# A two-layer graph network on one core: counts and column numbers in separate PSUM banks, one bank for transposes, own rows read a group earlier and transposed ahead of the sums

## The chip, the cores and the metric

The kernel runs on one core of a Trainium2 chip. The metric is the device time of one execution in microseconds (us); lower is better. The kernel is written so that the order of instructions on each engine is the order in the program; semaphores between the engines are put in by the framework wherever two instructions touch the same tile.

The core has a matrix engine (TensorE, "PE"), a vector engine (VectorE, "DVE"), a scalar engine (ScalarE, "ACT"), a general engine that here issues the indirect transfers (GpSimd, "POOL") and one that issues the plain transfers (SyncE, "SP"). TensorE writes into PSUM, which this kernel uses as eight banks of 128 partitions by 512 floats.

## The reference, cut to what matters

There are 6250 nodes with 512 floats each and 106250 directed edges `(src, dst)`: 50000 random pairs in both directions and a loop on every node, sorted by `dst`. Two layers follow each other:

```
layer 0:  out = segment_sum((x @ W_l.T + b_l)[src], dst) / max(deg, 1) + x @ W_r.T
          h   = layernorm(x + out)
layer 1:  msg = h[dst] @ W_neigh.T + b_neigh
          neigh = segment_sum(msg, src) / max(deg, 1)
          out = relu(h @ W_self.T + b_self + neigh)
          y   = layernorm(h + out) * gamma + beta
          result = layernorm(h + y)
```

Since the projection is linear, the kernel averages the neighbours' rows first and multiplies the average with the weights afterwards. Layer 1 sums by `src`, so its edges have to be sorted anew.

## The kernel before, in words

**Tiles and groups.** A layer's sorted edges are cut into 831 tiles of 128. Seven tiles (`SPAN`) form a window, which ends within 64 nodes (`H`); there are `NW` = 119 windows, and a visit to an eighth tile (`VIS` = 8), the last one of the window before, collects the edges at the border. A group `g` handles two windows, `g` and `Q + g` with `Q` = 60, in the lower and upper 64 partitions. The function `grouped` handles one layer with a loop over the groups and is called twice, for layer 0 with table `x` and for layer 1 with table `h_d`.

**The steps of a group**, with the lines of their instructions:

- `fetch(g)`: 14 indirect transfers on GpSimd (L478), each bringing the 128 rows of one tile, 256 KB, into `rows`. There are six such buffers of seven tiles, that is for three groups; the last tile of a group is read once more by the first sums of the next.
- `match(g)`: one VectorE instruction (L497, recorded at helper line L170) builds `hot`, which says for each edge of each visit which of the 64 nodes it belongs to, by comparing with the column numbers 0 to 63. These numbers lie in PSUM, in the first 64 columns of the tile `misc`.
- `shrink(g)`: ScalarE copies `hot` to the narrower type bf16, `hotb` (L504).
- `own_rows(g)`: SyncE loads two row numbers into registers (L509) and issues two transfers of the nodes' own rows into `own` (L543). In one group of layer 0 GpSimd gathers them.
- `visits(g)`: 16 TensorE matmuls sum the rows of each node in `agg` (L555).
- `count(g)`: eight small matmuls (L565) count the edges of each node, into column 64 or 65 of `misc`; VectorE forms `inv` and `some` from it (L438, L439, L441).
- `average(g)`: ScalarE multiplies `agg` by `inv` into `mean` (L574).
- `dense(g)`: 16 matmuls (L456) with both weights into `po`, of which there is one.
- `turn(g)`: TensorE transposes the own rows and then the averages, four blocks each (L447), into tiles `tp`, of which there are two; ScalarE copies each to `ownT` or `meanT` (L449).
- `store(g)`: the bias, the normalization and, in layer 1, the rest of the formula on VectorE (from L414 in layer 0, from L424 in layer 1; one square root on ScalarE, L406), then two transfers of the result by SyncE (L598).

**The order.** The program order of the loop sets the order on every engine. In round `g` it is: fetch and match of `g + 1`; own rows, visits, count and average of `g`; dense of `g - 1`; turn of `g`; store of `g - 1`; shrink of `g + 1`. In layer 0 the call `more` puts steps of the sort for layer 1 between these (five a round on VectorE, after the shrink; those with TensorE transposes after the average); groups 0 to 43 or so carry them, groups 44 to 59 none. Layer 1 has no such steps.

**PSUM.** The banks of a layer are one for `misc`, two for `tp`, two for `agg`, one for `po`, and two of the sort.

**Another path.** A function `plain` is there for edge lists that don't fit the windows. It uses the same `transposed` and doesn't run with these inputs.

Of the kernel before, what the change touches and what calls it, by code (L numbers as in the profile page):

```python
# [9 lines left out]
F32 = mybir.dt.float32  # L10
# [3 lines left out]
ALU = mybir.AluOpType  # L14
# [4 lines left out]
P = 128  # L19
H = 64  # L20
SPAN = 7
VIS = SPAN + 1
# [74 lines left out]
def kernel(  # L97
# [16 lines left out]
    nc = tc.nc  # L114
    N, D = x.shape
    E = src.shape[0]
    NK = D // P
# [16 lines left out]
    iota = const.tile([P, P], F32, name="iota")  # L134
# [33 lines left out]
    def both(o, a, b, op):  # L168

        nc.vector.scalar_tensor_tensor(o, a, 1.0, b, op0=ALU.mult, op1=op)  # L170
# [265 lines left out]
    def inverse(deg, nr, work):  # L436
        inv = work.tile([P, 1], F32, name="inv")
        nc.vector.tensor_scalar(inv[:nr], deg, 1.0, None, op0=ALU.max)  # L438
        nc.vector.reciprocal(inv[:nr], inv[:nr])  # L439
        some = work.tile([P, 1], F32, name="some")  # L440
        nc.vector.tensor_scalar(some[:nr], deg, 1.0, None, op0=ALU.min)  # L441
        return inv, some

    def transposed(v, nr, name, work, ps):
        p = ps.tile([P, NK, P], F32, name="tp", bufs=2)
        for k in range(NK):
            nc.tensor.transpose(p[:, k, :nr], v[:nr, k * P:(k + 1) * P], ident[:nr, :nr])  # L447
        t = work.tile([P, NK, P], F32, name=name)
        nc.scalar.copy(t[:, :, :nr], p[:, :, :nr])  # L449
        return t  # L450
# [9 lines left out]
    def grouped(s, table, w_n, w_s, layer, finish, dest, other, sps):  # L460


        with tc.tile_pool(name=f"g{layer}", bufs=2) as work, tc.tile_pool(
            name=f"gp{layer}", bufs=2, space=PSUM
        ) as ps:
            chunks, hots, state = {}, {}, {}
            misc = ps.tile([P, H + 2], F32, name="misc", bufs=1)
            nc.vector.tensor_copy(misc[:, :H], iota[:, :H])  # L468

            def halves(g):  # L470
                return [c for c in range(2) if c * Q + g < NW]

            def tiles(g, c):
                w = c * Q + g
                return range(w * SPAN, min(M, (w + 1) * SPAN))

            def gather(t, m):
                nc.gpsimd.indirect_dma_start(  # L478
                    out=t, out_offset=None, in_=table,
                    in_offset=bass.IndirectOffsetOnAxis(ap=s.idx[:, m:m + 1], axis=0))  # L480

            def fetch(g):
                if g == 0:

                    first = work.tile([P, D], F32, name="mean")
                    gather(first, Q * SPAN - 1)
                    chunks[-1, 1] = {Q * SPAN - 1: first}
                for c in halves(g):
                    t = work.tile([P, SPAN, D], F32, name="rows", bufs=CHUNKS)
                    chunks[g, c] = {}  # L490
                    for i, m in enumerate(tiles(g, c)):
                        gather(t[:, i, :], m)
                        chunks[g, c][m] = t[:, i, :]

            def match(g):
                hot = work.tile([P, VIS * 2, H], F32, name="hot")
                both(hot, s.rel[:, g].rearrange("p v c -> p (v c)").unsqueeze(2)  # L497
                     .to_broadcast([P, VIS * 2, H]),
                     misc[:, :H].unsqueeze(1).to_broadcast([P, VIS * 2, H]), ALU.is_equal)
                hots[g] = hot  # L500

            def shrink(g):
                hb = work.tile([P, VIS * 2, H], BF16, name="hotb", bufs=1)
                nc.scalar.copy(hb, hots[g])  # L504
                hots[g] = (hots[g], hb)

            def start(w, t):

                return nc.values_load(  # L509
                    s.lo_i[:1, w:w + 1], engines=[ENG.SP], min_val=0, max_val=t.shape[0] - H,  # L510
                    skip_runtime_bounds_check_because="the windows hold: N - H at most, or N "
                    "in a table of N + 128")

            def slots(g, beyond):

                n = H * len(halves(g))
                r = work.tile([P, 1], F32, name="r")
                for c in halves(g):
                    a, w = H * c, c * Q + g
                    nc.vector.tensor_scalar(r[a:a + H], slot[a:a + H], s.lo[a:a + H, w:w + 1],  # L520
                                            None, op0=ALU.add)
                    if beyond:
                        far = work.tile([P, 1], F32, name="far")
                        nc.vector.tensor_scalar(far[a:a + H], r[a:a + H],
                                                s.lo[a:a + H, w + 1:w + 2], FAR,
                                                op0=ALU.is_ge, op1=ALU.mult)
                        both(r[a:a + H], r[a:a + H], far[a:a + H], ALU.add)
                if not beyond:
                    nc.vector.tensor_scalar(r[:n], r[:n], float(N - 1), None, op0=ALU.min)
                i = work.tile([P, 1], I32, name="ri")  # L530
                nc.vector.tensor_copy(i[:n], r[:n])
                return i

            def own_rows(g):
                own = work.tile([P, D], F32, name="own")
                n = H * len(halves(g))
                if g == NW - 1 - Q and table.shape[0] < NP:
                    nc.gpsimd.indirect_dma_start(
                        out=own[:n], out_offset=None, in_=table,
                        in_offset=bass.IndirectOffsetOnAxis(ap=slots(g, False)[:n, :1], axis=0))  # L540
                    return own
                for c in halves(g):
                    nc.sync.dma_start(own[H * c:H * (c + 1)],  # L543
                                      table[ds(start(c * Q + g, table), H), :])
                return own

            def visits(g):
                agg = state[g]["agg"] = ps.tile([P, D], F32, name="agg")
                hot = hots[g][0]
                for v in range(VIS):  # L550
                    for c in halves(g):
                        w = c * Q + g
                        first, end = (1 if w == 0 else 0), 1 + len(tiles(g, c))
                        if first <= v < end:
                            nc.tensor.matmul(  # L555
                                agg[H * c:H * (c + 1), :], hot[:, 2 * v + c, :],
                                chunks[g if v else g - 1, c][w * SPAN + v - 1],
                                start=(v == first), stop=(v == end - 1))

            def count(g):  # L560
                st, hb = state[g], hots[g][1]
                nr = st["nr"]
                st["deg"] = misc[:, H + g % 2:H + g % 2 + 1]
                for v in range(VIS):
                    nc.tensor.matmul(st["deg"][:nr],  # L565
                                     hb[:, 2 * v:2 * v + nr // H, :].rearrange("p c h -> p (c h)"),
                                     ones_b, start=(v == 0), stop=(v == VIS - 1))
                st["inv"], st["some"] = inverse(st["deg"][:nr], nr, work)

            def average(g):  # L570
                st = state[g]
                nr = st["nr"]
                mean = work.tile([P, D], F32, name="mean")
                nc.scalar.mul(mean[:nr], st["agg"][:nr], st["inv"][:nr])  # L574
                st["mean"] = mean

            def turn(g):
                st = state[g]
                for v in ("own", "mean"):
                    st[v + "T"] = transposed(st[v], st["nr"], v + "T", work, ps)  # L580

            def dense(g):
                st = state[g]
# [21 lines left out]
            def more(count, tensor):  # L605

                while runs and count and runs[0][0] == tensor:
                    runs.pop(0)[1]()
                    count -= 1

            match(0)
            shrink(0)
            fetch(0)
            for g in range(Q + 1):


                if g + 1 < Q:
                    fetch(g + 1)
                    match(g + 1)
                if g < Q:  # L620
                    state[g] = {"nr": H * len(halves(g)), "own": own_rows(g)}
                    visits(g)
                    count(g)
                    average(g)
                    more(1, True)
                if g:
                    dense(g - 1)
                if g < Q:
                    turn(g)
                if g:  # L630
                    store(g - 1)
                if g + 1 < Q:
                    shrink(g + 1)
                more(5, False)
# [138 lines left out]
```

## Time and profile before

| quantity | value |
|---|---|
| median of 3 runs | 2681.61 us (2674.11 to 2683.77) |
| the profiled execution | 2719.07 us, its span 2717.3 us |
| granted TensorE clock in it, mean | 0.899 |
| PE, weight loads, DVE, ACT, POOL busy | 76%, 32%, 39%, 14%, 59% of the span |
| bytes moved | 508 MB, 187 GB/s on average |
| layer 0, groups with the sort (94 to 1045 us) | PE busy 755.5 of 950.7 us, clock 0.89 |
| layer 0, groups without (1063 to 1306 us) | PE busy 205.2 of 242.3 us, clock 0.99 |
| layer 1 (1433 to 2632 us) | PE busy 949.4 of 1199.5 us, clock 0.91 |

The profile follows one execution. Busy times are of the engines' own instructions, so an engine that is not busy may wait for a semaphore, issue a transfer or have nothing to do. In a group of instructions the number in the first column after the bar is their busy time in us, the next the mean of one in ns; after the second bar stands the idle time just ahead of them and what ended most of it. In a list of waits, each row names the waiting engine, what it was about to write, the instruction that released it, and the sum in us, the count and the longest. In the timeline, a row has the start and the busy time in us, the engine, the line and the operation; in square brackets stands the idle time ahead of it with its releaser.

### The profile page before, as it was taken

To read this page: it belongs to the slowest core of one execution; us is meant where nothing else is said; L and a number is where in the kernel's file an instruction comes from. 1 tells how busy PE (TensorE), PEld (TensorE's weight loads), DVE (VectorE), ACT (ScalarE), POOL (GpSimd) and SP (SyncE) were. 2 spreads that over 40 slices of the span, in tenths; PEclk is the share of its full clock that TensorE was granted. 3 is DMA by queue.
4 is the path that set the end of the run, shared out by engine and by line. 5 is a ranking of instruction groups with operands and counts; after the bars stand their busy time and mean duration, and the time that the engine had idled before them with its cause. 6 is when DMAs were issued, how large, how long until landed. Compare 5 with 4: busy or idle time off the path is not lost.

```text
span 2717.3 us, 23134 instructions
## 1 busy us (share of the span) xinstructions
PE 2071.7 (76%) x7807; PEld 861.5 (32%) x7807; DVE 1047.1 (39%) x2139; ACT 390.2 (14%) x685; POOL 1594.0 (59%) x1679
## 2 busy tenths in 40 slices
PE   2488887778787878888927777778777887877785
PEld 1133333333333333333303333333333333333332
DVE  1344434443434443222302444444444444444444
ACT  0111111111111111111101111111111111111111
POOL 4566665556666565666265566665666666656650
PEclk8789988888898989999968998999899899988998
DMA  7576766666666666676366666666666666666650
GB/s 225 164 204 192 204 199 187 184 182 190 190 191 192 184 196 185 196 214 207 106 178 175 189 192 199 202 201 197 187 202 199 203 200 187 195 189 196 202 174 19
DMA packets 177784, 508.07 MB, mean 187 GB/s; under 512 B 35564, under 2 KB 38054, under 8 KB 177646
## 3 DMA queue, kind: packets, MB, share of 16 engines
q0 software_dynamic: 133456, 437.13, 55.5%
q1 hardware_dynamic: 41358, 63.76, 7.3%
q10 hardware_dynamic: 2832, 5.51, 0.6%
q8 instruction: 66, 1.08, 0.2%
q14 instruction: 72, 0.59, 0.1%
HBM read 475.03 MB, written 31.46 MB: 186 GB/s over the span
## 4 chain that ended last, share of the span: by engine, by line
issue 23%; DVE 9%; PE 8%; SPq 7%; DMA 1%; ACT 1%; another core or an unknown queue 1%; POOLq 0%
PE po L456 6%; SPq L543 4%; SPq L598 2%; DVE po L170 2%; DVE stats L402 2%; SPq L509 2%; DVE po L408 1%; PE tp L447 1%; DVE po L424 1%; DVE po L427 1%; DMA own<-h_d 1%; DVE y L170 1%; PE agg L555 1%; ACT rstd L406 0%
## 5 line engine op out<-in xcount | busy, mean ns | idle before, releaser
L478 POOL DMA_INDIRECT rows<-in_x_dram,idx x831 | 797.0, 959 | 492.3 <-PE agg L555 240.3
L478 POOL DMA_INDIRECT rows<-h_d,idx x831 | 788.7, 949 | 482.5 <-PE agg L555 246.8
L555 PE MATMUL agg<-rows,hot 128*64 128x512 f32 x3792 | 918.2, 613 | 37.9 <-issue 21.7
L456 PE MATMUL po<-wb,ownT 128*128 128x512 f32 x960 | 574.2, 754 | 7.3 <-DVE y L170 6.3
L555 PEld LDWEIGHTS agg<-rows,hot 128*64 128x64 f32 x3792 | 293.8, 140 | 580.4 <-issue 536.8
L456 PE MATMUL po<-wa,meanT 128*128 128x512 f32 x960 | 431.5, 592 | 0.0
L565 PE MATMUL misc<-ones_b,hotb 128*128 128x1 bf16 x960 | 41.5, 164 | 349.1 <-issue 225.7
L456 PEld LDWEIGHTS po<-wb,ownT 128*128 128x128 f32 x960 | 222.2, 243 | 261.3 <-issue 260.1
L424 DVE SCALAR_TENSOR_TENSOR po<-bn,some,po 128x512 f32<-128x512 f32 (+1 forms) x60 | 45.3, 756 | 605.0 <-PE tp L447 264.0
L456 PEld LDWEIGHTS po<-wa,meanT 128*128 128x128 f32 x960 | 181.6, 189 | 234.0 <-issue 234.0
L449 ACT COPY ownT<-tp 128x512 f32<-128x512 f32 x120 | 69.9, 582 | 971.4 <-PE tp L447 497.6
L414 DVE SCALAR_TENSOR_TENSOR po<-bl_t,some,po 128x512 f32<-128x512 f32 (+1 forms) x60 | 45.2, 753 | 406.4 <-PE agg L555 212.9
L574 ACT ACTIVATE mean<-agg,inv 128x512 f32<-128x512 f32 x120 | 82.4, 687 | 788.9 <-DVE some L441 319.6
L438 DVE TENSOR_SCALAR inv<-misc 128x1 f32<-128x1 f32 x120 | 18.9, 158 | 425.7 <-remote 312.2
L170 DVE SCALAR_TENSOR_TENSOR srt<-srt 128x448 f32<-128x448 f32 (+2 forms) x310 | 180.2, 623 | 3.9
L565 PEld LDWEIGHTS <-hotb 128*128 128x128 bf16 x960 | 40.8, 99 | 443.9 <-issue 268.7
L447 PE MATMUL tp<-ident,mean 128*128 128x128 f32 x480 | 77.9, 288 | 123.0 <-ACT mean L574 112.1
L170 DVE SCALAR_TENSOR_TENSOR hot<-rel,misc 128x1024 f32<-128x1024 f32 x120 | 145.2, 1211 | 0.2 <-DVE misc L468 0.2
L447 PE MATMUL tp<-ident,own 128*128 128x128 f32 x480 | 76.0, 276 | 67.5 <-issue 39.3
L504 ACT CAST hotb<-hot 128x1024 bf16<-128x1024 f32 x120 | 123.5, 1029 | 22.6 <-DMA bn<-in_L_gnn_b_neigh_dram 16.1
L406 ACT ACTIVATE rstd<-mv,eps 128x1 f32<-128x1 f32 x180 | 53.0, 295 | 464.0 <-DVE mv L404 343.6
L447 PEld LDWEIGHTS tp<-ident,mean 128*128 128x128 f32 x480 | 58.9, 148 | 131.8 <-ACT mean L574 119.8
(111 smaller groups left out, 841.3 us busy)
## 6 DMA issues: line engine op xcount, KB each, us to landing
own<-h_d SPq DMA_DIRECT2D x119, 128.0 KB
own<-in_x_dram SPq DMA_DIRECT2D x117, 128.0 KB
h_d<-y SPq DMA_DIRECT2D x116, 128.0 KB
out_dram<-y SPq DMA_DIRECT2D x116, 128.0 KB
rows<-in_x_dram,idx POOLq DMA_INDIRECT x831
rows<-h_d,idx POOLq DMA_INDIRECT x831
wa<-in_L_gnn_W_l_dram ACTq DMA_DIRECT2D x1, 1024.0 KB
wb<-in_L_gnn_W_r_dram ACTq DMA_DIRECT2D x1, 1024.0 KB
```

Of the source, the lines that this page charges most:

```text
L170: nc.vector.scalar_tensor_tensor(o, a, 1.0, b, op0=ALU.mult, op1=op)
L402: nc.vector.bn_stats(stats[:nr], v)
L424: nc.vector.scalar_tensor_tensor(po, biases["bn"][:nr], some[:nr], po, op0=ALU.mult, op1=ALU.add)
L447: nc.tensor.transpose(p[:, k, :nr], v[:nr, k * P:(k + 1) * P], ident[:nr, :nr])
L449: nc.scalar.copy(t[:, :, :nr], p[:, :, :nr])
L456: nc.tensor.matmul(po[:nr], a[:, k, :nr], w[:, k, :], start=(i == 0 and k == 0), stop=(i == 1 and k == NK - 1))
L478: nc.gpsimd.indirect_dma_start(out=t, out_offset=None, in_=table, in_offset=bass.IndirectOffsetOnAxis(ap=s.idx[:, m:m + 1], axis=0))
L504: nc.scalar.copy(hb, hots[g])
L543: nc.sync.dma_start(own[H * c:H * (c + 1)], table[ds(start(c * Q + g, table), H), :])
L555: nc.tensor.matmul(agg[H * c:H * (c + 1), :], hot[:, 2 * v + c, :], chunks[g if v else g - 1, c][w * SPAN + v - 1], start=(v == first), st ...
L565: nc.tensor.matmul(st["deg"][:nr], hb[:, 2 * v:2 * v + nr // H, :].rearrange("p c h -> p (c h)"), ones_b, start=(v == 0), stop=(v == VIS - 1))
L574: nc.scalar.mul(mean[:nr], st["agg"][:nr], st["inv"][:nr])
```

## The change

The two parts of `misc` become two tiles, each with a bank of its own: `cols` for the column numbers that `match` reads, and `deg` for the counts. To make room, `tp` has one bank instead of two.

The own rows are asked for one group ahead: a new step `begin(g + 1)` follows `match(g + 1)`, and `own` has three buffers. In SyncE's order the reads of group `g + 1` now stand ahead of the stores of group `g - 1`; they stood behind those before. `turn` is split in two. The own rows of group `g` are transposed ahead of `visits(g)`; the averages are transposed where both were, after `dense(g - 1)`. `mean` has one buffer instead of two, and the single extra tile that a layer reads at its beginning goes into a buffer named `y` instead of `mean`.

```diff
 def transposed(v, nr, name, work, ps):
-    p = ps.tile([P, NK, P], F32, name="tp", bufs=2)
+    p = ps.tile([P, NK, P], F32, name="tp", bufs=1)
...
-            misc = ps.tile([P, H + 2], F32, name="misc", bufs=1)
-            nc.vector.tensor_copy(misc[:, :H], iota[:, :H])
+            cols = ps.tile([P, H], F32, name="cols", bufs=1)
+            nc.vector.tensor_copy(cols, iota[:, :H])
...
-                    first = work.tile([P, D], F32, name="mean")
+                    first = work.tile([P, D], F32, name="y")
...
-                     misc[:, :H].unsqueeze(1).to_broadcast([P, VIS * 2, H]), ALU.is_equal)
+                     cols.unsqueeze(1).to_broadcast([P, VIS * 2, H]), ALU.is_equal)
...
-                own = work.tile([P, D], F32, name="own")
+                own = work.tile([P, D], F32, name="own", bufs=3)
...
-                st["deg"] = misc[:, H + g % 2:H + g % 2 + 1]
+                st["deg"] = ps.tile([P, 1], F32, name="deg", bufs=1)
...
-                mean = work.tile([P, D], F32, name="mean")
+                mean = work.tile([P, D], F32, name="mean", bufs=1)
...
-            def turn(g):
+            def turn(g, v):
                 st = state[g]
-                for v in ("own", "mean"):
-                    st[v + "T"] = transposed(st[v], st["nr"], v + "T", work, ps)
+                st[v + "T"] = transposed(st[v], st["nr"], v + "T", work, ps)
...
+            def begin(g):
+                state[g] = {"nr": H * len(halves(g)), "own": own_rows(g)}
+
             match(0)
             shrink(0)
             fetch(0)
+            begin(0)
             for g in range(Q + 1):
                 if g + 1 < Q:
                     fetch(g + 1)
                     match(g + 1)
+                    begin(g + 1)
                 if g < Q:
-                    state[g] = {"nr": H * len(halves(g)), "own": own_rows(g)}
+                    turn(g, "own")
                     visits(g)
                     count(g)
                     average(g)
                     more(1, True)
                 if g:
                     dense(g - 1)
                 if g < Q:
-                    turn(g)
+                    turn(g, "mean")
                 if g:
                     store(g - 1)
```

## The prediction

> **What bounds the kernel now.** I read the engine shares first, then the costliest groups, the releasers of idle time, and then single groups of edges in the timeline. TensorE is busy 76% of the span and ends no chain alone; GpSimd, which issues the gathers, is busy 59%.
>
> Costliest groups (busy us, mean ns of one; idle us before them, and what ended most of it):
>
> ```profile
> L478 POOL DMA_INDIRECT rows<-h_d,idx x831 | 788.7, 949 | 482.5 <-PE agg L555 246.8
> ...
> L555 PE MATMUL agg<-rows,hot 128*64 128x512 f32 x3792 | 918.2, 613 | 37.9 <-issue 21.7
> ...
> L565 PE MATMUL misc<-ones_b,hotb 128*128 128x1 bf16 x960 | 41.5, 164 | 349.1 <-issue 225.7
> ...
> L449 ACT COPY ownT<-tp 128x512 f32<-128x512 f32 x120 | 69.9, 582 | 971.4 <-PE tp L447 497.6
> ```
>
> A gather is 0.95 us of work and 0.30 of issue, so the 14 of a group need 14 x 1.25 = 17.5 us, and from the first one's start to the last one's end 17.2. The waits by engine (sum us, count, longest) say what the idle GpSimd, ScalarE and TensorE wait for:
>
> ```profile
> ACT ownT L449 <- PE tp L447: 497.6, 56, 10.7
> POOL rows L478 <- PE agg L555: 487.0, 109, 11.8
> DVE inv L438 <- remote: 312.2, 25, 58.8
> PE misc L565 <- DVE hot L170: 122.2, 36, 9.9
> PE tp L447 <- DMA own<-h_d: 27.0, 20, 2.5
> ```
>
> The last two are what the change can take away: the count waits for the match of the next group only because both touch one bank, and the transposes wait for their own rows. The first three don't fit the engines' busy times, and the timeline shows why. A layer 0 group without sorting (start us, busy us):
>
> ```profile
> 1157.42 3.60 PE L456 MATMUL po<-wa,meanT 128*128 128x512 f32 x8
> ...
> 1165.69 0.95 POOL L478 DMA_INDIRECT rows<-in_x_dram,idx  x1 [0.30 <-issue]
> ...
> 1169.46 0.76 DVE L414 SCALAR_TENSOR_TENSOR po<-bl_t,some,po 128x512 f32<-128x512 f32 x1 [13.86 <-PE agg L555]
> 1169.52 0.58 ACT L449 COPY ownT<-tp 128x512 f32<-128x512 f32 x1 [13.19 <-PE agg L555]
> 1169.88 0.94 POOL L478 DMA_INDIRECT rows<-in_x_dram,idx  x1 [3.25 <-PE agg L555]
> ```
>
> The dense sum ends at 1161.0. VectorE, idle and waiting for it alone, answers at 1169.5, when the last gather of the running stream has landed (its issue ended at 1166.6, plus 2.9). ScalarE's copy and the next stream start in the same instant. Following all 109 dense ends: 99 fall inside a stream, and 97 of these are answered only 2.5 us or more after the last gather's end (median 2.96); the ten that fall later are answered in 0.04 us. So **TensorE's completions reach the other engines late while a gather stream runs, and come out when it has landed**. An idle TensorE doesn't release them, as layer 0 with sorting shows:
>
> ```profile
> 806.55 0.34 PE L565 MATMUL misc<-ones_b,hotb 128*128 128x1 bf16 x8 [0.43 <-issue]
> ...
> 816.67 0.95 POOL L478 DMA_INDIRECT rows<-in_x_dram,idx  x1 [0.30 <-issue]
> ...
> 820.60 0.16 DVE L438 TENSOR_SCALAR inv<-misc 128x1 f32<-128x1 f32 x1 [14.09 <-remote]
> 821.04 0.69 ACT L574 ACTIVATE mean<-agg,inv 128x512 f32<-128x512 f32 x1 [19.08 <-DVE some L441]
> 821.79 1.12 PE L447 MATMUL tp<-ident,mean 128*128 128x128 f32 x4 [5.86 <-ACT mean L574]
> ```
>
> The count ends at 806.9, TensorE is idle from 815.9, and the inverse starts at 820.6, 3 us after the last gather's end. A stream itself starts on the first sums of a group, so the period locks to 17.2 + 2.9 + 0.35 = 20.45 us in layer 0 without sorting (20.2 to 20.45 measured); with sorting it is 22.2 and in layer 1 21.4 (starts of groups, averaged).
>
> **What the Trainium skill says.** (1) "Perfetto Trace Analysis", Per-instruction lifecycle (Tensor Engine Instruction): a matmul's end is estimated, and its semaphore update follows PSUM's acknowledgement, outside the window shown. The trace fits: the answer takes 0.04 us at best and 14 at worst. (2) "PSUM — Partial Sum Buffer", PSUM bank collisions: two engines in one bank are ordered by bank, not address. That is the wait "PE misc <- DVE hot" above. (3) "Perfetto Trace Analysis", Optimizing Tensor Performance, Matmuls: independent groups should rotate through banks so that evacuation overlaps the next group. Before, the two transposes run 0.46 us apart (2007.59 and 2008.05 in layer 1); after, one bank serves both. (4) "TensorE: Matmul & The Clock Gate", What's actually happening: an idle window of some 3.4 us halves the clock. The trace agrees: dense matmuls stand 0.43 us apart, and 0.85 after long idle.
>
> **The change part by part.** The instructions are the same in number on every engine; only places and waits change.
>
> *Separate banks.* Layer 1's count loses its wait for the match, which stands on VectorE behind the 8.8 us finish: some 3.5 us of TensorE a group. The new bank for counts waits only for the inverse of the group before, over long ago. Costed at nothing beyond that.
>
> *Own rows one group ahead.* The two reads of the next group and their register loads now stand on SyncE in front of a store instead of behind it; they land 3.6 to 4.5 us after issue, and the third buffer gives them some 20 us. The wait of 0 to 3 us (0.8 to 1 on average in layer 1) goes. The stores come later by two issues, which nothing waits for. Nothing further; without that cover of a period it would be the landing, up to 4.5 us a group. In layer 0's group 58 own rows are one GpSimd gather with index steps on VectorE: once, some 2 us moved, nothing. The averages' single buffer: the older one has been transposed before it is rewritten, nothing.
>
> *Own transposes ahead of the sums, one bank.* Together these two gains would take 4 to 5 us off TensorE's layer 1 group, and 1 more by keeping its clock. But here a wait is added. The own transposes of group g+1 overwrite the bank that holds the mean transposes of g, so TensorE must wait for ScalarE's copy of these. Queued behind the waiting transpose are the sums of g+1, and on their first signal hangs the next stream. The mean transposes end 14 to 16 us into the stream, so their completion is held to its landing. Counted from the stream's first gather:
>
> - stream and landing 17.2 + 2.9 = 20.1
> - copy: answer 0.05, copy 0.58
> - own transposes: answer 0.05; 1.0 after 5 us of idle (0.5 at full clock; 1.12 is the row at 821.79)
> - first sums to their signal: 2.3 at half clock, 1.35 at full (both read from the starts of streams)
>
> The sum is 24.1 at half clock, 22.65 at full. I take 24.0, since the idle of 5 us is longer than what halves the clock. The 56 + 56 periods between groups 1 and 57 of layer 0 and of layer 1 take 1214 + 1199.5 = 2413.5 us before. 112 x 24.0 = 2688, so **+275 us**. What lies outside (layer ends, opening streams, first sort: 306 us) I leave. The profiled execution took 2719.07 us (span 2717.3), above the median of 2681.61 by 37; I add the 275 to each: 2994 and **2957, say 2960**. With 22.65 to 25.0 a period (the upper end where a third of the counts is held too, see below) this case reaches from 2805 to 3070.
>
> Bounds of the unknown: the new wait was never in the trace. From below, it costs a prompt round trip: 0.05 + 0.58 + 0.05 = 0.7 us; from above, the hold to landing for the count as well. I take the hold of one signal, because 97 of 99 dense ends, the ones nearest in place, show it.
>
> **The rivals.**
>
> *The round trip is prompt (ends faster).* If TensorE, stopped at the bank, has its last signal out at once, the trip costs 0.7 us against 4 to 5 saved; TensorE then needs 7.1 (sums) + 0.34 + 7.0 (dense) + 1.0 + 0.7 = 16.1 us and the stream sets 20.45, as in layer 0 without sorting. 112 x 20.45 = 2290, so -123: 2560 (2520 to 2640). For it: counts with 2.5 us of idle TensorE ahead were answered in 0.04. Against it: the row at 820.60. It decides from the point where the copy starts less than 3 us after the mean transposes' end.
>
> *The count is held too (slower still).* Layer 1's idle ahead of the count goes with the match's wait. Of 16 counts without idle ahead, the lag was 1 to 14.5 us, median 7.5, and six were held to the landing. If all are, the inverse starts at 20.1, then 0.45 to the mean, 0.7 for it, 1.1 transposes, then the trip of 4.0: 26.4, with answers 26.8; 112 x 26.8 = 3002, +588: 3270. A third of them gives 25.
>
> *No hold at all.* If the late answers came from the order of work before, GpSimd's 17.5 us become the bound: 1960, -454: 2230 to 2280. Against it: nothing in the change touches the streams.
>
> *It does nothing*: the waits saved and added balance, 2670 to 2690.
>
> **How the numbers follow.** Hold of one signal 0.52 (2960), count held too 0.16 (3070 to 3270), prompt 0.22, no hold 0.06, balance 0.04. A measurement of this kernel can tell about 0.5% from no change. Faster 0.28, same 0.04, slower 0.68. Both signs hold much of the chance: the likeliest one's own range is 2805 to 3070; the range of 2540 to 3100 leaves out the free case, the lowest of the prompt one and most of the held counts, some 0.17.
>
> **What the profile after would show.** Right: a wait of the own transposes for ScalarE's copy of the mean's, 4 to 6 us in some 110 groups; that copy starting about 3 us after the last gather's end; GpSimd idle ended by the first sums of 24.0 - 17.5 = 6.5 us a group, against 487.0/109 = 4.5 now; no wait of the count for the match, none for own rows. Wrong: copies that start at once after the mean transposes, with GpSimd idle of 4 us a group or less.

## The result and the profile after

The changed kernel takes 2983.53 us (2979.9 to 2986.35, four runs) against 2682.36 before (four runs): 1.1129 times as long, with a 95% interval of 1.1103 to 1.1155. Its profiled execution took 2986.35 us, the span is 2984.5, and the mean granted clock fell from 0.899 to 0.849. Times here are medians of all runs and ratios are of the fast runs alone, which matters for one kernel below, where 4 of 19 runs lay over 1.5% above its fastest.

The costliest groups of the page of the changed kernel, to be held against those of before:

```profile
L478 POOL DMA_INDIRECT rows<-h_d,idx x831 | 787.3, 947 | 622.4 <-PE agg L555 386.5
L555 PE MATMUL agg<-rows,hot 128*64 128x512 f32 x3792 | 1072.9, 723 | 7.3 <-DMA rows<-h_d,idx 5.0
L447 PE MATMUL tp<-ident,own 128*128 128x128 f32 x480 | 129.7, 423 | 650.9 <-ACT meanT L449 619.6
...
L449 ACT COPY meanT<-tp 128x512 f32<-128x512 f32 x120 | 69.9, 582 | 671.3 <-remote 622.6
```

A gather still takes 0.95 us, but GpSimd's idle ahead of layer 1's gathers rose from 482.5 to 622.4 us. The own transposes, cheap before, stand behind 650.9 us of idle. The count's row is no longer among the costliest. The list of waits says who releases whom (sum us, count, longest; "remote" is a releaser that the list could not name):

```profile
POOL rows L478 <- PE agg L555: 769.5, 113, 13.9
DVE inv L438 <- remote: 700.0, 81, 59.3
...
ACT meanT L449 <- remote: 622.6, 100, 11.7
PE tp L447 <- ACT meanT L449: 619.6, 116, 7.6
```

Two waits of before are gone: the count's for the match (122.2 us) and, but for one at the start of each layer, the transposes' for own rows (27.0 us). In their place TensorE waits 116 times, 5.3 us each, for ScalarE's copy. A layer 1 group in the timeline (start, busy us) shows what that copy waits for:

```profile
2102.67 0.35 PE L565 MATMUL deg<-ones_b,hotb 128*128 128x1 bf16 x8
...
2109.51 0.16 DVE L438 TENSOR_SCALAR inv<-deg 128x1 f32<-128x1 f32 x1 [8.09 <-remote]
...
2110.73 0.66 PE L447 MATMUL tp<-ident,mean 128*128 128x128 f32 x4 [0.73 <-issue]
2111.63 0.95 POOL L478 DMA_INDIRECT rows<-h_d,idx  x1 [0.30 <-issue]
2115.26 0.76 DVE L424 SCALAR_TENSOR_TENSOR po<-bn,some,po 128x512 f32<-128x512 f32 x1 [5.33 <-remote]
2115.32 0.59 ACT L449 COPY meanT<-tp 128x512 f32<-128x512 f32 x1 [4.64 <-remote]
...
2115.95 1.11 PE L447 MATMUL tp<-ident,own 128*128 128x128 f32 x4 [4.57 <-ACT meanT L449]
...
2117.00 9.63 PE L555 MATMUL agg<-rows,hot 128*64 128x512 f32 x32
...
2119.24 0.95 POOL L478 DMA_INDIRECT rows<-h_d,idx  x1 [6.66 <-PE agg L555]
```

The mean transposes end at 2111.4. The last gather's issue ends at 2112.6, and 2.7 us later VectorE and ScalarE, both idle, start 0.06 us apart. Only then come the own transposes, the sums at half clock, and, 2.24 us into them, the next stream.

Only TensorE is answered late. Of 59 hand-overs from VectorE to ScalarE (L404 to L406) inside the streams of this kernel 58 took 0.04 us or less, and so did all 58 from ScalarE back to VectorE (L406 to L407). And it is at least in part the signal that is late, not the matmul: of 109 groups in which both the dense sums and the mean transposes are answered over 1 us late, 96 have the two answers less than 0.1 us apart, while the four transposes, all behind the dense sums, take 0.33 us from the first start to the last (median).

Averaged over groups, in us (layer 0 with sorting, without, layer 1):

| kernel | layer 0, sort | layer 0, no sort | layer 1 |
|---|---|---|---|
| before | 22.2 | 20.2 | 21.4 |
| changed | 24.1 | 23.7 | 23.9 |

The 112 periods that the prediction used took 1345.0 + 1335.7 = 2680.7 us, against 2413.5 before: 267.2 us more, which is the whole difference of the spans (2984.5 - 2717.3).

### The profile page after: what moved, and what is told of

Its sections match the earlier page's. It is cut to its first block, busy times and chain, and to the rows that moved or that the text cites. A ratio compares the mean times of both kernels' runs of the same rounds, so it can differ in the third digit from the quotient of the medians.

```text
span 2984.5 us, 23135 instructions
## 1 busy us (share of the span) xinstructions
PE 2155.7 (72%) x7807; PEld 852.3 (29%) x7807; DVE 1054.4 (35%) x2139; ACT 390.4 (13%) x685; POOL 1590.7 (53%) x1679
## 5 line engine op out<-in xcount | busy, mean ns | idle before, releaser
L478 POOL DMA_INDIRECT rows<-h_d,idx x831 | 787.3, 947 | 622.4 <-PE agg L555 386.5
L555 PE MATMUL agg<-rows,hot 128*64 128x512 f32 x3792 | 1072.9, 723 | 7.3 <-DMA rows<-h_d,idx 5.0
L447 PE MATMUL tp<-ident,own 128*128 128x128 f32 x480 | 129.7, 423 | 650.9 <-ACT meanT L449 619.6
L555 PEld LDWEIGHTS agg<-rows,hot 128*64 128x64 f32 x3792 | 313.0, 167 | 699.5 <-issue 615.2
L456 PE MATMUL po<-wb,ownT 128*128 128x512 f32 x960 | 444.9, 606 | 13.3 <-DVE y L170 6.4
L438 DVE TENSOR_SCALAR inv<-deg 128x1 f32<-128x1 f32 x120 | 19.0, 158 | 917.0 <-remote 700.0
L447 PEld LDWEIGHTS tp<-ident,own 128*128 128x128 f32 x480 | 83.2, 212 | 680.6 <-ACT meanT L449 647.7
L456 PEld LDWEIGHTS po<-wb,ownT 128*128 128x128 f32 x960 | 173.3, 190 | 191.6 <-issue 183.7
L449 ACT COPY meanT<-tp 128x512 f32<-128x512 f32 x120 | 69.9, 582 | 671.3 <-remote 622.6
L170 DVE SCALAR_TENSOR_TENSOR hot<-rel,cols 128x1024 f32<-128x1024 f32 x120 | 144.6, 1206 | 0.3 <-DVE cols L468 0.3
L504 ACT CAST hotb<-hot 128x1024 bf16<-128x1024 f32 x120 | 123.5, 1029 | 22.7 <-DMA ga<-in_L_gnn_ln_gamma_dram 16.1
L406 ACT ACTIVATE rstd<-mv,eps 128x1 f32<-128x1 f32 x180 | 53.0, 294 | 526.7 <-DVE mv L404 362.0
```

Of the source, the lines that this page charges most:

```text
L406: nc.scalar.activation(rstd[:nr], mv[:nr, 1:2], AF.Sqrt, bias=eps[:nr])
L456: nc.tensor.matmul(po[:nr], a[:, k, :nr], w[:, k, :], start=(i == 0 and k == 0), stop=(i == 1 and k == NK - 1))
L478: nc.gpsimd.indirect_dma_start(out=t, out_offset=None, in_=table, in_offset=bass.IndirectOffsetOnAxis(ap=s.idx[:, m:m + 1], axis=0))
L555: nc.tensor.matmul(agg[H * c:H * (c + 1), :], hot[:, 2 * v + c, :], chunks[g if v else g - 1, c][w * SPAN + v - 1], start=(v == first), st ...
```

## The experiments

A stream is the run of 14 gathers of one group; it has landed when its last rows are in SBUF. "The trip" is the round trip TensorE, ScalarE, TensorE through the one bank for transposes. The theory: the trip costs the loss, because its first signal comes out only when the stream has landed. The rivals: the place of the own transposes or reads costs by itself; TensorE's answers are late in any case, whatever GpSimd does; the bytes in flight make them late. The kernel before took 2676 to 2710 us on the chips used, so single times are read to about 1%.

### One bank or place

Two banks for transposes, with column numbers and counts back in one:

```diff
-    p = ps.tile([P, NK, P], F32, name="tp", bufs=1)
+    p = ps.tile([P, NK, P], F32, name="tp", bufs=2)
...
-            cols = ps.tile([P, H], F32, name="cols", bufs=1)
+            misc = ps.tile([P, H + 2], F32, name="misc", bufs=1)
```

> The changed kernel with two banks for transposes again, the column numbers and counts back in one bank; own rows still asked for a group ahead and transposed ahead of the sums. Theory (the round trip through the one bank, whose completion is held to the stream's landing, costs the whole loss): the trip is gone, groups of layer 0 without sorting at 20.2 to 20.5 us, layer 1 at 20.5 to 21.4 (its count waits for the match again, its own rows are there): 2620 to 2690 us. Rival (the place of the own transposes ahead of the sums, or the own reads ahead of the stores, costs by itself): stays above 2900.

Measured: 2717.41 us beside 2709.8 for the kernel before on that chip, ratio 1.0028 (1.0007 to 1.0049). The loss is gone, so the rival of the place falls: transposes and reads stand where the change put them. (That the counts share a bank again is not what removed it: the kernel with columns in SBUF below leaves the counts their own bank.) But the small gain expected beside it is missing: the forecast was 2620 to 2690. Layer 0 without sorting is at 20.1 us and layer 1 at 21.6, where 20.5 to 21.4 was forecast. Layer 1's count still waits. The waits of this kernel:

```profile
PE misc L565 <- issue: 150.8, 47, 8.1
...
PE misc L565 <- ACT ownT L449: 112.8, 28, 5.8
PE misc L565 <- DVE hot L170: 87.8, 31, 7.0
```

Having its own rows earlier only moved TensorE's wait to the count.

The single bank kept, the own transposes back at their old place:

```diff
-                    turn(g, "own")
                     visits(g)
...
+                    turn(g, "own")
                     turn(g, "mean")
```

> The changed kernel with the own transposes back at their old place, after the dense sums and right ahead of the averages' transposes, still with one bank. Theory: the round trip now lies between the two transposes, 14 us into the stream, and is held to the landing just as before: 23.5 to 24.5 us a group, 2940 to 3020 us. Rival (the place costs, not the bank): 2600 to 2700.

Measured: 2999.22 us, 23.9 us a group without sorting and in layer 1. The trip has moved between the two transposes and costs the same. Its row in the list of waits:

```profile
PE tp L447 <- ACT ownT L449: 741.6, 118, 40.0
```

So it is the bank, and the place of the own transposes ahead of the sums is not needed for the loss.

### Is it the stream that holds

Tiles 1, 3 and 5 of each half's seven are not gathered:

```diff
-                        gather(t[:, i, :], m)
-                        chunks[g, c][m] = t[:, i, :]
+                        if i % 2 == 0:
+                            gather(t[:, i, :], m)
+                        chunks[g, c][m] = t[:, i - i % 2, :]
```

That leaves 8 gathers of 14, not the 7 that the expectations name, and a stream of 9.7 us.

> The kernel before with 7 of the 14 gathers of each group left out (the sums read the neighbouring tile's rows instead, so they are other sums of the same size). The stream takes 8.4 us and lands 2.9 us later, at 11.3, ahead of the dense sums' end. Theory (completions are held by the stream): nothing is held there any more, TensorE's own work of 15.5 us and its wait for the match (3 to 4 us in layer 1) set 16 to 19 us a group: 2080 to 2300 us. Rival (TensorE's answers are some 5 us late whatever the stream does): 20 to 22 us a group, above 2450.

> The changed kernel with the same 7 gathers of each group left out. Theory: the averages' transposes end after the landing, their completion comes at once, the round trip costs 0.7 us, and the wait for the match is gone: 16 to 17.5 us a group, 2080 to 2250 us, and so from 50 us slower to 150 us faster than the kernel before with the same gathers left out, where with all gathers it is 300 us slower. Rival (the trip is 5 us long by itself): 20 to 22 us a group, and 300 us or more slower than the kernel before with the same gathers left out.

Measured: 2224.21 us for the kernel before and 2101.5 for the changed one. **The order turns round**: with fewer gathers the change is 123 us faster. All mean transposes now end after the landing (typically 4 us after the last gather's end, with the landing at 2.7), and in the timeline of the changed kernel so thinned the copy follows at once:

```profile
2014.00 0.60 PE L447 MATMUL tp<-ident,mean 128*128 128x128 f32 x4
2014.63 0.58 ACT L449 COPY meanT<-tp 128x512 f32<-128x512 f32 x1 [2.28 <-PE tp L447]
2015.27 0.66 PE L447 MATMUL tp<-ident,own 128*128 128x128 f32 x4 [0.68 <-ACT meanT L449]
```

The trip is the 0.7 us that the prediction gave as its lower bound. The layers show both sides of the change. Layer 1 falls from 17.7 to 16.4 us a group, because the kernel before still waits for the match there (144.4 us, 61 times); layer 0 without sorting, which has no such wait, rises from 15.2 to 16.1. For the trip, a lateness of TensorE's own, whatever the stream does, is ruled out.

The opposite: two gathers more in each group (the first tile of each half once more).

```diff
                         chunks[g, c][m] = t[:, i, :]
+                    if 0 < g < Q - 1:
+                        gather(t[:, 0, :], tiles(g, c)[0])
```

> The kernel before with 2 gathers more in each group (the first tile of each half is read once more at the half's end). Theory: the stream takes 2.5 us more and the hold ends so much later: 22.9 us a group where it was 20.4, and 22.9 to 23.9 in layer 1: 2840 to 2990 us. Rival (TensorE's lateness is its own): GpSimd needs 20.0 of the 20.2 to 22 us of a group, so little changes: 2680 to 2760.

> The changed kernel with the same 2 gathers more in each group. Theory: the copy that TensorE waits for starts 2.5 us later in the group, 26.3 us a group where it was 23.9: 3230 to 3290 us. Rival (TensorE's lateness is its own): GpSimd has 6.5 us of idle in a group that take up the 2.5, so nothing changes: 2970 to 3020.

Measured: 2949.08 us for the kernel before (23.3 us without sorting, 23.7 in layer 1) and 3325.6 for the changed one (26.7 and 26.9). GpSimd had 6.8 us of idle a group to absorb 2.5 us, and absorbed nothing; the group grew by 3.0. The forecast of 3230 to 3290 was 36 us short: the copy now starts 3.2 us after the last gather's end (median) instead of 2.7. TensorE's wait for the copy grew by 2.6 us, to 917.2/116 = 7.9:

```profile
PE tp L447 <- ACT meanT L449: 917.2, 116, 13.2
```

The same number of gathers, with rows of 512 bytes instead of 2 KB:

```diff
+            quarters = table.rearrange("n (a b) -> (n a) b", a=NK)
...
-                    out=t, out_offset=None, in_=table,
+                    out=t[:, :P], out_offset=None, in_=quarters,
...
-                                chunks[g if v else g - 1, c][w * SPAN + v - 1],
+                                chunks[g if v else g - 1, c][w * SPAN + v - 1][:, :P]
+                                .unsqueeze(1).to_broadcast([P, NK, P]),
```

> The changed kernel with all 14 gathers a group, each with 128 rows of 512 bytes instead of 2 KB (the sums read the 128 columns four times, so they are other sums of the same size). GpSimd issues as long as before, the bytes are a quarter. If completions are held by gathers that are under way, whatever their size, the copy that TensorE waits for still starts 2 to 3 us after the last gather's end and the group takes 23 to 24 us: 2880 to 3000 us. If the bytes moved (contention with the writes of the rows) make TensorE's answers late, they come within 1 us, the wait of the own transposes falls below 1.5 us, and GpSimd sets the group: 17.5 to 20.5 us, 2260 to 2600.

Measured: 2985.76 us. With a quarter of the bytes nothing moved: 23.8 us a group in layer 1, a gather still 0.945 us, the copy 2.73 us after the last gather's end (median, as in the changed kernel). TensorE's wait:

```profile
PE tp L447 <- ACT meanT L449: 602.3, 115, 7.7
```

Contention by the bytes is ruled out, and with it the landing as what lets the signals go. In the packets of this trace the last rows of a stream arrive 1.25 us after the last gather's end (median; 2.40 in the changed kernel), and the copy still starts at 2.7: 107 of the 109 late copies start after the landing, 1.5 us in the median. One group of layer 1:

```profile
2111.06 0.94 POOL L480 DMA_INDIRECT rows<-h_d,idx  x1 [0.30 <-issue]
2114.71 0.59 ACT L449 COPY meanT<-tp 128x512 f32<-128x512 f32 x1 [4.58 <-remote]
```

The stretches between the two, with the busy times of the engines, the clock, the DMA share and GB/s:

```profile
2112.00:2113.30 1.30, 0.00 (x0) 0.00 (x0) 0.00 (x0) 0.00 (x0) 0.00 (x1) 1.00 0.20 50
2113.30:2114.70 1.40, 0.00 (x0) 0.00 (x0) 0.05 (x1) 0.00 (x0) 0.00 (x0) 1.00 0.00 0
```

In the second nothing is moved any more, and ScalarE still waits. So in both kernels the hold ends some 2.7 us after the last gather's issue on GpSimd, whether the rows came just before (2 KB) or 1.5 us before (512 bytes); with 16 gathers it was 3.2, with the rows there at 2.4. Where the landing is named as the end of the hold, the runs show this moment instead. What GpSimd does in these 2.7 us the profile does not show.

### Keeping the gain without the loss

The own transposes between count and dense sums:

```diff
-                    turn(g, "own")
                     visits(g)
                     count(g)
+                    turn(g, "own")
```

> The changed kernel with the own transposes between the count and the dense sums, still with one bank, so that 7 us of dense sums lie between them and the averages' transposes. If every completion inside a stream is held to its landing, the averages' transposes wait to 20.7 us after the stream's first gather, and the group takes 23.5 to 24.5 us again: 2940 to 3020. If early completions come out in mid-stream, as the counts' do in the changed kernel (5 to 6 us after the count's end, 11 to 14 us into the stream), the copy is done before the dense sums end and the group takes 20.5 to 21.5: 2560 to 2700.

Measured: 2642.09 us, beside 2709.8 for the kernel before on that chip. One bank is enough if the trip lies beside 7 us of dense sums and starts early in the stream. It was timed again:

> The kernel with the own transposes between count and dense sums once more, timed against the kernel before: 20.2 us a group in layer 0 without sorting, 21.1 with it and 20.8 in layer 1 as in its first run, so 1.5 to 3.5% faster than the kernel before, 2610 to 2660 us.

Measured: 2604.1 us beside 2676.51, ratio **0.9741 (0.9719 to 0.9764)**: faster than both kernels, and 6 us below the forecast range. Groups take 20.6, 20.3 and 20.5 us (in the order of the table), near the period that the stream and the lag behind it set (17.3 + 2.7 + 0.3 = 20.3 from this trace). No wait of TensorE for ScalarE's copy is left in its list. Its timeline in layer 1:

```profile
2103.34 0.60 PE L447 MATMUL tp<-ident,mean 128*128 128x128 f32 x4
...
2107.62 0.58 ACT L449 COPY meanT<-tp 128x512 f32<-128x512 f32 x1 [6.88 <-remote]
2107.90 0.95 POOL L478 DMA_INDIRECT rows<-h_d,idx  x1 [3.37 <-remote]
...
2116.81 1.09 PE L447 MATMUL tp<-ident,own 128*128 128x128 f32 x4
...
2122.12 0.58 ACT L449 COPY ownT<-tp 128x512 f32<-128x512 f32 x1 [5.61 <-remote]
```

The copy of the averages is still held, here 3.7 us, but TensorE is at its sums meanwhile, and GpSimd restarts 0.3 us after it. The own copy comes 4.2 us late, in mid-stream, under the dense sums.

From here, own rows asked for in their own group again:

```diff
                     match(g + 1)
-                    begin(g + 1)
                 if g < Q:
+                    begin(g)
                     visits(g)
```

> The kernel with the own transposes between count and dense sums, but the own rows asked for in their own group, behind the store, as in the kernel before. Theory: the count and the own transposes now come 7 to 8 us after the group's start, and the rows land about 7 us after the store at the start, so TensorE waits 0 to 4 us for them ahead of the dense sums, whose end is held to the landing anyway: 0 to 1.5 us a group more than with the reads a group ahead, 2640 to 2800 us. Rival (the early reads, being ahead of the stores, cost something themselves): 2560 to 2640.

Measured: 3183.15 us, ratio 1.1896 (1.1871 to 1.1921) to the kernel before: far outside my range. Layer 0 loses 1.6 to 1.8 us a group, layer 1 takes 28.6 us. Its timeline shows a loop that I had not seen:

```profile
2495.89 0.75 DVE L424 SCALAR_TENSOR_TENSOR po<-bn,some,po 128x512 f32<-128x512 f32 x1 [17.42 <-PE po L456]
...
2504.72 1.54 SPq L597 DMA_DIRECT2D out_dram<-y  x2
2509.83 4.31 SPq L543 DMA_DIRECT2D own<-h_d  x2
...
2515.57 1.09 PE L447 MATMUL tp<-ident,own 128*128 128x128 f32 x4 [10.32 <-issue]
...
2525.96 0.76 DVE L424 SCALAR_TENSOR_TENSOR po<-bn,some,po 128x512 f32<-128x512 f32 x1 [19.27 <-PE po L456]
```

The store waits 8.8 us for VectorE's finish, the read is issued 5.1 us behind the store, the transposes start 5.7 us later, and the next finish follows 10.4 us after them: 30.1 us for this group, 28.6 in the mean. With the own transposes ahead of the dense sums the early read is needed to keep the gain.

The columns from SBUF, so that counts get a bank and transposes two:

```diff
-            cols = ps.tile([P, H], F32, name="cols", bufs=1)
-            nc.vector.tensor_copy(cols, iota[:, :H])
...
-                     cols.unsqueeze(1)
+                     iota[:, :H].unsqueeze(1)
...
-    p = ps.tile([P, NK, P], F32, name="tp", bufs=1)
+    p = ps.tile([P, NK, P], F32, name="tp", bufs=2)
```

> The changed kernel with the column numbers read from SBUF instead of PSUM, which frees a bank: the counts have their own bank and the transposes two. Theory: no trip and no wait for the match, the period is what the stream and its landing set, 20.2 to 20.7 us in all groups but those with sorting: 2540 to 2640. Rival (with both operands in SBUF the match, or the gathers beside it, get slower by more than a microsecond a group; or the hold of the count, with no idle of TensorE ahead of it, lengthens the group): 2650 to 2800.

Measured: 2697.91 us, ratio 0.9929 (0.9901 to 0.9957), not the 2540 to 2640 of the theory. The loss is gone here too, with the counts in a bank of their own. Layer 1 takes 20.8 us a group, layer 0 with sorting 21.9. Part of what is missing is in the gathers, as the rival had it: in layer 1 the 112 of 831 that run beside a match take 1.26 us in the mean, against 0.95 in the changed kernel. The other 719 are unchanged at 0.947, and so is the match itself (1.22 us). Together that makes 0.989 a gather, and a stream of 17.9 us instead of 17.2. By which path the match slows the gathers beside it was not tried.

Last, row buffers that come free earlier, through a copy of each half's last tile:

```diff
+            def carry(g):
+                cr = state["carry"] = work.tile([P, 2, D], F32, name="carry", bufs=1)
...
+                        nc.scalar.copy(cr[:, c, :], chunks[g, c][m])
...
                     average(g)
+                    carry(g)
```

> The kernel with the own transposes between count and dense sums, and the last tile of each half copied by ScalarE into a small buffer for the next group's first sums, so that a row buffer comes free at the end of its group's sums, some 13 us earlier, and GpSimd needn't wait for the next group's first sums (own rows and results in one buffer less, for the space). If completions come out in mid-stream even while streams follow each other without a pause, GpSimd's 17.5 us set the group: 17.5 to 19 us, 2260 to 2480 us. If they come out at landings only, two streams run together and TensorE stops at its next round trip until both have landed: 20 to 22 us a group, 2580 to 2820.

Measured: 2829.7 us, 22.3 us a group in layer 1, 10 us above the range of the second alternative. It doesn't answer its question. ScalarE's copy stands behind that of the own rows; these come late, probably for want of the third buffer that was given up for space, and GpSimd waits for both. The waits:

```profile
POOL rows L478 <- ACT carry L567: 495.4, 90, 17.0
...
PE tp L447 <- DMA own<-h_d: 100.0, 33, 4.2
```

Whether streams without a pause could beat 20.4 us a group stays open.

## Why the prediction was right

- **The new wait.** Forecast: 4 to 6 us in some 110 groups. Measured: 5.3 us, 116 times. GpSimd's idle for the first sums was forecast at 6.5 us a group and is 6.8.
- **The hold.** Forecast: the copy starts about 3 us after the last gather's end. Measured: 2.7 us in the median; of 109 mean transposes done inside a stream one was answered within a microsecond. Thinning and lengthening the stream move the hold with it. What ends it was read wrongly: the prediction says the landing, and with rows of 512 bytes the rows land at 1.25 us and the signal still comes at 2.7. That the sum came out with the landing in it was luck; with 2 KB rows the two moments lie 0.3 us apart.
- **The sum.** Forecast: 24.0 us a group. Measured: 23.9, with the own transposes at 1.1 and the sums' first signal at 2.24. The half clock is part of it, as the forecast had it.
- **What was left alone.** Outside the 112 periods lie 303.8 us of the span before and after. (The prediction's 306 takes the time of the execution, 2719.07, where the periods are read from the span, 2717.3.) The counts' bank, the own rows and the averages' buffer cost nothing that shows.
- **The gain that was to be there.** The waits for match and own rows are gone, and two experiments show a gain: 1.2 us a group in layer 1 with 8 gathers, and with all 14 and the own transposes after the count 0.9 in layer 1 (21.4 to 20.5), 1.6 in layer 0 with sorting and none without. The forecast of 4 to 5 us counted TensorE's idle, of which most only stood beside the stream.
- **The own rows' cover.** Forecast: without it up to 4.5 us a group. In the order with own transposes ahead of the dense sums it was 8.1 in layer 1 (28.6 against 20.5): the landing alone was counted, and not the loop through the store.
- **The rival of the prompt trip** is what the kernels with 8 gathers do. **The held counts** did not come: of 111 counts in the changed kernel, one was held to the landing; the others came out in mid-stream, 4.6 us late in layer 0 and 5.6 in layer 1 (medians). Six of the 16 cases without idle ahead, taken from the kernel before, misled here.
- **The one term that was off.** The profile was forecast at 2994 and took 2986, 8 us less. The median was forecast at 2960 and is 2983.5. The profiled execution of before lay 37 us above its median; that of the changed kernel only 3 above its own. Adding the difference of two profiles to a median carries this scatter along.

What stays open is the path by which GpSimd's gathers hold TensorE's signals, what happens in the 2.7 us after the last of them, why early signals come out in mid-stream, and how much of the lateness is the matmul's: "Perfetto Trace Analysis", Per-instruction lifecycle, of the Trainium skill says that a matmul's end is an estimate. The answers 0.06 us apart show that the signal is late, but not that the matmuls end when the trace says.

## What to carry to other kernels

Before taking a buffer away, ask which signal its reuse waits for, when in the period that signal is sent, and what stands queued behind the waiting instruction. Here one round trip cost 0.7 us or 5.3, depending only on what another engine was doing; placed early and under 7 us of other work it cost nothing that shows. The Trainium skill's advice to rotate matmul groups through banks ("Perfetto Trace Analysis", Optimizing Tensor Performance, Matmuls) could be broken without loss there, and nowhere else that was tried.

## What was not expected

The hold depends neither on the bytes nor on their landing: a gather of 128 rows of 512 bytes took 0.945 us and held the signals as long as one of 2 KB rows, though its rows were there 1.2 us sooner. And a match that read both operands from SBUF, no slower itself, made the gathers beside it 0.31 us longer and left the others as they were, 0.6 us a stream.
